# Keys, values and context of the first layer moved beside the edge checks, and the last layer's matrices loaded inside the edge loop of a graph transformer

## The chip, the cores and the metric

The kernel runs on one core of one Trainium2 chip. The metric is the device time of one execution in microseconds (us); lower is better. Engines are called by short names: PE is TensorE, DVE is VectorE, ACT is ScalarE, POOL is GpSimd and SP is SyncE, which here only issues transfers.

## The reference

Four layers work on 3125 nodes of 256 features with 103125 directed edges (`src`, `dst`, sorted by `dst`). Each layer adds a graph attention, a global mixing and an expert network:

```python
xn = layernorm(x)
x = x + gnn_i(xn, src, dst) + mix_i(xn)
x = x + ffn_i(layernorm(x))
```

The change touches the mixing and the edge attention of layer 0 and the expert network of layer 3:

```python
# layer 0, mixing: linear attention with a gate
q, k, v = split(x @ Wqkv)                      # 8 heads of 32
k = softmax(k, over the nodes)
context = einsum('nhd,nhv->hdv', k, v)
out = einsum('nhd,hdv->nhv', q, context)
gate = sigmoid(gelu((layernorm(x) * g + b) @ Wg1 + bg1) @ Wg2 + bg2)
mix = out * gate @ Wproj + bproj
# layer 0, edges: softmax over the edges of a target of leaky_relu(s_src[src] + s_trg[dst]),
# weighted sum of proj[src]
# layer 3, experts: one of 8 by the largest gate
H = gelu(x @ W1 + b1)                          # 1024 features
probs = softmax(H @ Wg + bg)
out[n] = probs[n, e] * (H[n] @ Wd[e] + bd[e])  # e = argmax(probs[n])
```

`Wd` is 8 matrices of 1024 x 256, 8.4 MB in f32.

## The kernel before

Nodes lie in 25 tiles of 125 (`NT`, `TP`), with 7 groups of three or four tiles (`GROUPS`). `x`, its layernorm `xn` and the transposed `xT` stay on chip through the whole kernel. All matrices are f32.

**Start.** `begin_layer` loads and normalises `x` group by group on DVE and ACT and turns it on PE. Then `prepare` checks whether the edges have the properties that the fast path needs (segments of the edge list per node block, sortedness, a bound on the attention exponents): five scans of 3224 numbers over `heads` on DVE (L1357), their addresses `at_i` (L1360), five indirect gathers on POOL, a DVE chain on the gathered segments, and matmuls `p_e` on every group of `xT` for the bounds of the attention scores. It ends in one number, `ok`, which every engine reads to choose a branch (`layers` or `general`). Only then does layer 0's real work start.

**Layer 0.** The attention of layers 0 to 2 is done densely, by a matrix of edge counts, `count_d`, in DRAM. `counts` makes it in 63 steps: per step DVE builds two one-hot tensors (`oh_lo` L1491, `oh_key` L1494), PE multiplies them into `p_cnt` and ACT copies the counts to a stage that SP stores. Between the steps it draws pieces of other work from a generator, so many that `PIECES0` pieces are spread over the steps:

```python
while done < (g0 // B + 1) * PIECES0 // steps:
    next(work, None)
    done += 1
```

What is left over follows after the last step. The pieces come from `mix0_pieces`, in this order: the loads of layer 0's weights and a POOL addition of `bproj` to all of `x`; 25 pieces of keys, values and context (per tile a product `p_a` with half of `Wqkv`, an exponential `ek` and a copy `v` on ACT, a column of ones on POOL, and two products into the running `p_ctx`); the folding of the context into the query matrix (`fold`); per group a normalised `xnn`, its turned `xnnT` with `ln_g` and `ln_b` (DVE, L1576), the gate (L1592) and the projection, added to `x` (L1599); then `node_pieces` for the edge attention's node terms: `hg` and its store `q_g`, `zs` and `es`, the exponentials `bar` and `es`, and last the scaling of `zs` by `es` on DVE. The dense attention (`pt` L1675, `acc`) then reads `count_d` and `q_g` back (`a`, `q_head`).

**Layer 3.** Its attention goes edge by edge in 101 steps (`edge_attention`): gathers of source rows on POOL, row and edge data on SP, one-hot products on PE. It too draws pieces: first the mixing `mix3`, then for each group the hidden layer `hidden3`, which writes each node's 1024 hidden features to `hid_d`. After the loop `routed3` loads `w_d`, one transfer an expert on SP, sorts the nodes by expert (`route`, whose result is `node_of`), gathers tiles of 128 nodes of one expert (`hid_tile` L2244), turns them (`p_t`) and multiplies by the expert's matrix (`p_q`).

The order of work on each engine is the order of the program, with the tiles' buffers as the only other limit.

Of the kernel before, what the change touches and what calls it, by code (L numbers as in the profile page):

```python
# [10 lines left out]
F32 = mybir.dt.float32  # L11
# [4 lines left out]
AF = mybir.ActivationFunctionType  # L16
OP = mybir.AluOpType
AX = mybir.AxisListType
PSUM = bass.MemoryType.PSUM
DRAM = bass.MemoryType.DRAM  # L20

P = 128
N = 3125
TP = 125
NT = N // TP
C = 256
KC = C // P
# [14 lines left out]
KEYS = HI * GN  # L42
PIECES0 = 107
SC = 8
# [5 lines left out]
GROUPS = [(0, 4), (4, 4), (8, 4), (12, 4), (16, 3), (19, 3), (22, 3)]  # L50
# [1276 lines left out]
class Dense(Net):  # L1327
# [8 lines left out]
    def prepare(self, pool, xT):  # L1336
# [6 lines left out]
        with ExitStack() as s:  # L1343
# [18 lines left out]
            for b in range(GN):  # L1362
                nc.gpsimd.indirect_dma_start(out=seg[:, b, :], out_offset=None, in_=ins["segments"],
                                             in_offset=bass.IndirectOffsetOnAxis(ap=at_i[:, b:b + 1], axis=0))
            lo = w.tile([TP, GN, SEG], F32, name="seg_lo")
            key = w.tile([TP, GN, SEG], F32, name="seg_key")
# [37 lines left out]
            nc.vector.tensor_reduce(found[:, 1:2], above, AX.X, OP.add)  # L1404
            p_f = ps.tile([1, 2], F32, name="p_f")
            nc.tensor.matmul(p_f, self.ones[:, 0:1], found, start=True, stop=True)


            gw = self.gnn_weight(w, ps, "g0", 8)
            ends = w.tile([16, 2, len(GROUPS)], F32, name="ends")  # L1410
# [30 lines left out]
            nc.vector.tensor_mul(self.ok, ok[:, 0:1], ok[:, 2:3])  # L1441
        return self.ok

# [4 lines left out]
    def counts(self, pieces):  # L1448
# [5 lines left out]
        with ExitStack() as s:  # L1454
# [5 lines left out]
            with tc.tile_pool(name="cnti", bufs=1) as wi, tc.tile_pool(name="cntt", bufs=2, space=PSUM) as ps:  # L1460
                for i, name in enumerate(("lo_t", "key_t")):
# [12 lines left out]
                    by_edge.append(t)  # L1474
            ps = s.enter_context(tc.tile_pool(name="cntp", bufs=3, space=PSUM))
            lo_t, key_t = by_edge
# [42 lines left out]
    def mix0_pieces(self, x, xn, xT, nodes, c, w):  # L1519
# [3 lines left out]
        with ExitStack() as s:  # L1523
            ps = s.enter_context(tc.tile_pool(name="m0p", bufs=3, space=PSUM))
            ps1 = s.enter_context(tc.tile_pool(name="m0p1", bufs=1, space=PSUM))
            wqkv = self.weight(c, "L0_mix_Wqkv")
            wproj = self.weight(c, "L0_mix_Wproj")
# [3 lines left out]
            bg1, bg2 = self.vec(c, "L0_mix_bg1", rows=64), self.vec(c, "L0_mix_bg2")  # L1531
            bproj = self.row(c, "L0_mix_bproj")
            nc.gpsimd.tensor_add(x, x, bproj[:, None, :].to_broadcast([TP, NT, C]))
            p_ctx = [ps1.tile([P, P + 1], F32, name=f"p_ctx{m}") for m in range(KC)]
            yield
            for t in range(NT):
                p = ps.tile([TP, 2 * C], F32, name="p_a")
                self.mm(p, [(xT[:, k, t * TP:(t + 1) * TP], wqkv[:, k, C:]) for k in range(KC)])
                ek = w.tile([TP, C], F32, name="ek", bufs=2)
                nc.scalar.activation(ek, p[:, :C], AF.Exp)  # L1540
                v = w.tile([TP, KC, P + 1], F32, name="v", bufs=2)
                nc.scalar.activation(v[:, :, :P], p[:, C:].rearrange("p (m f) -> p m f", m=KC), AF.Copy)
                nc.gpsimd.memset(v[:, :, P], 1.0)
                for m in range(KC):
                    nc.tensor.matmul(p_ctx[m], ek[:, m * P:(m + 1) * P], v[:, m, :], start=(t == 0), stop=(t == NT - 1))
                yield

            inv = w.tile([P, KC], F32, name="inv")
            ctxt = w.tile([P, KC, P], F32, name="ctxt")
            for m in range(KC):  # L1550
                nc.vector.reciprocal(inv[:, m:m + 1], p_ctx[m][:, P:])
                nc.vector.scalar_tensor_tensor(ctxt[:, m, :], p_ctx[m][:, :P], inv[:, m:m + 1], self.heads, op0=OP.mult, op1=OP.mult)
            fold = c.tile([P, KC, C], F32, name="fold")
            for k in range(KC):
                p = ps.tile([P, 512], F32, name="p_a")
                for m in range(KC):
                    nc.tensor.transpose(p[:, m * P:(m + 1) * P], wqkv[:, k, m * P:(m + 1) * P], self.ident)
                wt = w.tile([P, C], F32, name="wq_t")
                nc.vector.tensor_copy(wt, p[:, :C])
                p = ps.tile([P, 512], F32, name="p_a")  # L1560
                for m in range(KC):
                    nc.tensor.matmul(p[:, m * P:(m + 1) * P], wt[:, m * P:(m + 1) * P], ctxt[:, m, :], start=True, stop=True)
                nc.vector.tensor_copy(fold[:, k, :], p[:, :C])
            yield
            for t0, nt in GROUPS:
# [6 lines left out]
                for k in range(KC):  # L1572
                    p = ps.tile([P, 512], F32, name="p_a")
                    for t in range(nt):
                        nc.tensor.transpose(p[:, t * TP:(t + 1) * TP], xnn[:, t, k * P:(k + 1) * P], self.ident[:TP, :TP])
                    nc.vector.tensor_scalar(xnnT[:, k, :n], p[:, :n], g[:, k:k + 1], b[:, k:k + 1], op0=OP.mult, op1=OP.add)  # L1576
                yield
# [580 lines left out]

    def hidden3(self, w, ps, x, xn, xT, t0, nt, weights, ones, hid_d):

# [4 lines left out]
        n = nt * TP  # L2165
        cs = slice(t0 * TP, t0 * TP + n)
        mv = w.tile([TP, nt, 2], F32, name="mv")
# [7 lines left out]
        for t in range(nt):  # L2175
            nc.vector.tensor_scalar(xn[:, t0 + t, :], x[:, t0 + t, :], mv[:, t, 0:1], rstd[:, t:t + 1],
                                    op0=OP.subtract, op1=OP.mult)
        yield
        for k in range(KC):
            p = ps.tile([P, 512], F32, name="p_h")  # L2180
            for t in range(nt):
                nc.tensor.transpose(p[:, t * TP:(t + 1) * TP], xn[:, t0 + t, k * P:(k + 1) * P], self.ident[:TP, :TP])
            nc.scalar.activation(xT[:, k, cs], p[:, :n], AF.Copy)
            yield
        h = w.tile([P, F, 3 * TP], F32, name="h")
        for f in range(F):
            p = ps.tile([P, 512], F32, name="p_h")
            self.mm(p[:, :n], [(w1[:, k, f * P:(f + 1) * P], xT[:, k, cs]) for k in range(KC)])
            nc.scalar.activation(h[:, f, :n], p[:, :n], AF.Gelu, bias=b1[:, f:f + 1], scale=1.0)
            if f % 2:  # L2190
                yield
# [29 lines left out]

    def routed3(self, ones, hid_d, out):

# [6 lines left out]
        with ExitStack() as s:  # L2230
            c = s.enter_context(tc.tile_pool(name="r3", bufs=1))
            wd = c.tile([P, F, E, C], F32, name="w_d")
            for e in range(E):
                nc.sync.dma_start(wd[:, :, e, :], self.ins["L3_ffn_Wd"][e].rearrange("(k p) f -> p k f", p=P))
            bd = self.matrix_rows(c, "L3_ffn_bd")
            node, to, mats = self.route(c, ones, NJ)
            wd2 = wd.rearrange("p k e f -> p k (e f)")
            w = s.enter_context(tc.tile_pool(name="r3x", bufs=3))
# [17 lines left out]
            def products(j):  # L2256
                mat[j] = nc.values_load(mats[0:1, j:j + 1], engines=(mybir.EngineType.PE, mybir.EngineType.DVE), min_val=0, max_val=(E - 1) * C)
                q = ps.tile([P, C], F32, name="p_q")
                self.mm(q, [(hts[j][:, f, :], wd2[:, f, bass.ds(mat[j], C)]) for f in range(F)])
                y = w.tile([P, C], F32, name="y_tile")  # L2260
                nc.vector.tensor_add(y, q, bd[:, bass.ds(mat[j], C)])
                nc.vector.scalar_tensor_tensor(y, y, hrs[j][:, HID:HID + 1], hrs[j][:, HID + 1:], op0=OP.mult, op1=OP.add)
                self.scatter(y_d, to, j, y, "y3")
# [155 lines left out]
    def run(self, x_in, out):  # L2419
# [3 lines left out]
        x = pool.tile([TP, NT, C], F32, name="x")  # L2423
        xn = pool.tile([TP, NT, C], F32, name="xn")
        xT = pool.tile([P, KC, N], F32, name="xT")
# [3 lines left out]
        out_v = out.rearrange("(t p) c -> p t c", p=TP)  # L2429
        self.begin_layer(x, xn, xT)  # L2430
        ok = nc.values_load(self.prepare(pool, xT)[0:1, 0:1], min_val=0, max_val=1)
        with tc.If(ok > 0) as either:
# [4 lines left out]
    def layers(self, x, xn, xT, out):  # L2437
# [32 lines left out]
        with tc.tile_pool(name="layer3", bufs=1) as lp:  # L2470
            ones = lp.tile([TP, NT, 8], BF16, name="one_e")
            hid_d = self.dram.tile([N, HID + 1 + C], F32, name="hid_d")
            with tc.tile_pool(name="edges", bufs=1) as ep:
                with tc.tile_pool(name="ffn2", bufs=1) as wp:
# [6 lines left out]
                self.edge_attention(  # L2481
                    x, xT, edge, lambda w, ps: self.mix3(w, ps, x, xn, xT, mix),
                    lambda w, ps, t0, nt: self.hidden3(w, ps, x, xn, xT, t0, nt, hid, ones, hid_d))
            self.routed3(ones, hid_d, out)

# [127 lines left out]
```

## Time and profile before

| | us |
|---|---|
| median of 3 runs | 5581.91 (5577.47 to 5591.57) |
| the profiled execution | 5581.36, its span 5579.3 |
| PE busy | 4887.1 (88%) |
| DVE busy | 3778.7 (68%) |
| ACT busy, POOL busy | 1037.5 and 1038.3 (19% each) |
| start to the branch on `ok` | 93.9 |
| first and last step of the counting | 131.3 to 385.4 |
| first `pt` of the dense attention | 406.33 |
| edge loop of layer 3 | 4299 to 5361 |
| first `p_q` of layer 3's experts | 5418.31 |

The granted clock of PE was 0.935 on average. Busy times are sums over the whole span; a share of 88% is an average over stages that have different limits, so the rows below it, the places where one stage ends and the next starts, are what a change to one stage is read against. A row of the timeline gives start, length, engine, line, operation and tiles, and in brackets how long the engine was idle before it and what released it.

### The profile page before, as it was taken

What the parts mean: (1) busy time and instruction counts of PE and PEld (TensorE: products, weight loads), DVE (VectorE), ACT (ScalarE), POOL (GpSimd) and SP (SyncE); (2) the same over time, 40 slices, a digit from 0 to 9 for tenths busy, and PEclk for the clock granted to TensorE, in tenths of its full rate; (3) what the DMA queues carried; (4) which work ended last, traced back from release to release, by engine and by line L of the source; (5) the groups of instructions that cost most, each with busy time, mean ns of one, the idle gap of its engine ahead of it and who ended that gap; (6) DMA issues with size and microseconds to landing.
All of it is one profiled execution on the core that took longest, in us unless ns stands there. A gap on an engine that the chain in (4) does not pass through costs nothing. (4 is left out here: it accounts for less than half of the span.)

```text
span 5579.3 us, 66975 instructions
## 1 busy us (share of the span) xinstructions
PE 4887.1 (88%) x24880; PEld 2854.4 (51%) x24880; DVE 3778.7 (68%) x6022; ACT 1037.5 (19%) x1991; POOL 1038.3 (19%) x1184
## 2 busy tenths in 40 slices
PE   3978888879698899999999899979998888988868
PEld 2652234448555433378544433345565556655557
DVE  7789999975555699745443899932223888777743
ACT  2540010011143100100123000023233112332221
POOL 1000000004200000000001100000001777767733
PEclk7989999979899999999889999979999889999989
DMA  3462222232300011111000011120002556666655
GB/s 87 35 69 66 77 63 66 67 114 65 111 1 1 29 34 41 30 41 36 19 1 4 28 33 34 33 63 0 1 0 65 158 156 179 180 167 169 179 168 170
DMA packets 294389, 395.84 MB, mean 71 GB/s; under 512 B 124223, under 2 KB 228048, under 8 KB 293483
## 3 DMA queue, kind: packets, MB, share of 16 engines
q1 hardware_dynamic: 205646, 163.34, 12.5%
q0 software_dynamic: 52528, 167.17, 10.6%
q10 hardware_dynamic: 35882, 60.93, 3.4%
q8 instruction: 203, 3.33, 0.3%
q14 instruction: 130, 1.06, 0.1%
HBM read 345.14 MB, written 49.35 MB: 71 GB/s over the span
## 5 line engine op out<-in xcount | busy, mean ns | idle before, releaser
L1675 DVE SCALAR_TENSOR_TENSOR pt<-q_head,bar,a 128x750 f32<-128x750 f32 (+5 forms) x1200 | 1483.5, 1299 | 80.3 <-PE acc L1780 57.3
L1930 POOL DMA_INDIRECT z_edge<-tab,src_i x806 | 775.0, 962 | 274.5 <-issue 207.9
L1724 PE MATMUL acc<-pt,zs 128*64 128x500 f32 (+2 forms) x2800 | 592.1, 549 | 150.7 <-DVE pt L1675 126.7
L1775 PE MATMUL acc<-pt,zs 128*64 128x375 f32 (+2 forms) x3200 | 605.9, 502 | 25.2 <-DVE pt L1675 24.9
L1998 PE MATMUL p_acc<-z_edge,oh 128*125 128x264 f32 x2044 | 542.4, 427 | 94.9 <-DVE z_edge L1989 94.8
L1998 PEld LDWEIGHTS p_acc<-z_edge,oh 128*125 128x125 f32 x2044 | 421.1, 210 | 195.3 <-DVE z_edge L1989 105.1
L1724 PEld LDWEIGHTS acc<-pt,zs 128*64 128x64 f32 (+1 forms) x2800 | 244.8, 137 | 482.7 <-DVE pt L1675 327.0
L1775 PEld LDWEIGHTS acc<-pt,zs 128*64 128x64 f32 (+1 forms) x3200 | 245.1, 136 | 362.7 <-issue 224.5
L1191 DVE SCALAR_TENSOR_TENSOR x<-p_y,sm,x 125x256 f32<-125x256 f32 x200 | 93.9, 484 | 428.2 <-PE p_y L716 428.2
L1780 PE MATMUL acc<-pt,zs 128*32 128x375 f32 (+2 forms) x3200 | 313.4, 497 | 0.0
L1826 PE MATMUL acc<-zs,pt 128*125 128x257 f32 x1250 | 275.7, 383 | 11.6 <-issue 11.6
L1826 PEld LDWEIGHTS acc<-zs,pt 128*125 128x125 f32 x1250 | 234.8, 189 | 52.5 <-issue 14.4
L1989 DVE TENSOR_TENSOR z_edge<-z_edge,near_e 128x2112 f32<-128x2112 f32 (+1 forms) x101 | 236.6, 2342 | 16.7 <-ACT near_e L1981 16.7
L1186 ACT ACTIVATE h<-p_tr,bn 128x500 f32<-128x500 f32 (+1 forms) x224 | 161.5, 722 | 361.1 <-PE p_tr L716 361.1
L716 PE MATMUL p_y<-w_L_ffn_Wo,h 128*125 128x256 f32 x800 | 203.7, 387 | 0.0
L1675 DVE SCALAR_TENSOR_TENSOR pt<-q_all,bar,a 128x500 f32<-128x500 f32 (+3 forms) x175 | 119.1, 682 | 122.6 <-PE acc L1826 120.3
L1622 POOL MEMSET es<- 128x4 f32 (+2 forms) x4 | 1.6, 400 | 1052.1 <-PE acc L1780 723.3
L716 PE MATMUL p_tr<-h,w_L_ffn_W 128*128 128x500 f32 (+1 forms) x448 | 191.7, 551 | 6.3 <-ACT h L1186 3.2
L716 PE MATMUL p_tr<-xT,w_L_ffn_W 128*128 128x500 f32 (+1 forms) x448 | 193.0, 554 | 0.0
L2315 POOL CAST one_e<-one 125x96 bf16<-125x96 f32 (+1 forms) x2 | 2.1, 1047 | 1014.0 <-DVE one L653 1014.0
L1780 PEld LDWEIGHTS acc<-pt,zs 128*32 128x32 f32 (+1 forms) x3200 | 85.0, 109 | 203.1 <-issue 201.8
L716 PEld LDWEIGHTS p_y<-w_L_ffn_Wo,h 128*125 128x125 f32 x800 | 144.9, 187 | 73.5 <-ACT h L1186 27.1
(505 smaller groups left out, 6998.5 us busy)
## 6 DMA issues: line engine op xcount, KB each, us to landing
row<-dst_row SPq DMA_DIRECT2D x101, 224.0 KB
a<-count_d SPq DMA_DIRECT2D x96, 203.1 KB
a<-count_d SPq DMA_DIRECT2D x96, 187.5 KB
a<-count_d SPq DMA_DIRECT2D x144, 93.8 KB
ef<-in_edge_s SPq DMA_DIRECT2D x101, 128.0 KB
z_edge<-tab,src_i POOLq DMA_INDIRECT x806
count_d<-stage SPq DMA_DIRECT2D x12, 781.2 KB
q_head<-q_g ACTq DMA_DIRECT2D x24, 375.0 KB
```

Source lines behind the costliest of these rows:

```text
L716: self.nc.tensor.matmul(p, a, b, start=(i == 0), stop=(i == len(pairs) - 1))
L1186: nc.scalar.activation(o[:, m, :n], p[:, :n], AF.Relu, bias=b[:, e, m:m + 1], scale=g[:, e, m:m + 1])
L1191: nc.vector.scalar_tensor_tensor(x[:, t0 + t, :], q, wf[:, t, e:e + 1], x[:, t0 + t, :], op0=OP.mult, op1=OP.add)
L1675: self.nc.vector.scalar_tensor_tensor(pt[:K, :n], q, bar, a[:K, :n], op0=OP.max, op1=OP.mult)
L1724: nc.tensor.matmul(acc[64 * i:64 * i + 64, :b1 - b0], zs[:K, t, z:z + 64], pts[i][:K, b0:b1], start=(t == 0), stop=(t == NS - 1))
L1775: nc.tensor.matmul(acc[i // 2][64 * (i % 2):64 * (i % 2) + 64, b, :b1 - b0], zs[:K, t, i * W:i * W + 64], pts[i][:K, b0:b1], **st)
L1780: nc.tensor.matmul(acc[2][32 * i:32 * i + 32, b, :b1 - b0], zs[:K, t, z:z + 32], pts[i][:K, b0:b1], **st)
L1826: nc.tensor.matmul(acc[i], pt[:K, i * TP:(i + 1) * TP], zs[:K, t, :C + 1], start=(t == 0), stop=(t == NS - 1))
L1930: nc.gpsimd.indirect_dma_start(out=zs[i][:, j, :], out_offset=None, in_=table, in_offset=bass.IndirectOffsetOnAxis(ap=src[:, c0 + j:c0 + j ...
L1989: nc.vector.tensor_mul(zh, zh, weight[:, :, :, None].to_broadcast([P, n, H, D + 1]))
L1998: nc.tensor.matmul(acc[t], ohs[i, t][:, k - a, :], zs[i][:, k - c0, :HW], start=(k == cols[t][0]), stop=(k == cols[t][1] - 1))
L2315: nc.gpsimd.tensor_copy(ones[:, 0, ts, :], one1)
```

## The change

There are two independent parts.

1. Layer 0's keys, values, context and fold move into a new function, `begin`, ahead of the branch: `begin_layer` is gone from the start, and each group's layernorm, turning and key/value products follow each other, while `prepare` becomes a generator that stops twice, once behind the segment gathers and once ahead of its last matmuls. The fold goes through DRAM (`fold_d`) to the pieces. `PIECES0` falls from 107 to 69, while the pieces fall from 107 to 81, so that the last twelve (the end of `node_pieces`) follow the counting. `xnnT` is written by ACT instead of DVE, and two PSUM pools get four buffers instead of three.
2. `Wd` is loaded in eight parts by rows of 128 hidden features (1 MB each) instead of by expert. Five of them go on SP inside the edge loop, as ten more pieces behind `mix3`, into the space of `xT` and `xn`; `hidden3` uses a small remainder of `xn` for its own normalised and turned tiles. The other three follow in `routed3`, two on ACT's queue and one on SP's, and the bias `bd` behind them.

```diff
-PIECES0 = 107
+PIECES0 = 69
...
                 nc.gpsimd.indirect_dma_start(out=seg[:, b, :], out_offset=None, in_=ins["segments"],
                                              in_offset=bass.IndirectOffsetOnAxis(ap=at_i[:, b:b + 1], axis=0))
+            yield
...
             nc.vector.tensor_reduce(found[:, 1:2], above, AX.X, OP.add)
+            yield
-            p_f = ps.tile([1, 2], F32, name="p_f")
+            p_f = ps.tile([1, 2], F32, name="p_e")
...
+    def begin(self, pool, x, xn, xT):
...
+            checks = self.prepare(pool, xT)
+            next(checks)
+            wqkv = self.weight(c, "L0_mix_Wqkv")
+            p_ctx = [ps1.tile([P, P + 1], F32, name=f"p_ctx{m}") for m in range(KC)]
+            self.layernorm(xn, x, GROUPS[0])
+            for i, (t0, nt) in enumerate(GROUPS):
+                self.transposed(pst, xT, xn, groups=[GROUPS[i]])
+                if i + 1 < len(GROUPS):
+                    self.layernorm(xn, x, GROUPS[i + 1])
+                if i == 2:
+                    next(checks)
+                for t in range(t0, t0 + nt):
+                    p = ps.tile([TP, 2 * C], F32, name="p_a")
+                    self.mm(p, [(xT[:, k, t * TP:(t + 1) * TP], wqkv[:, k, C:]) for k in range(KC)])
+                    ek = w.tile([TP, C], F32, name="ek")
+                    nc.scalar.activation(ek, p[:, :C], AF.Exp)
+                    v = w.tile([TP, KC, P + 1], F32, name="v")
+                    nc.scalar.activation(v[:, :, :P], p[:, C:].rearrange("p (m f) -> p m f", m=KC), AF.Copy)
+                    nc.gpsimd.memset(v[:, :, P], 1.0)
+                    for m in range(KC):
+                        nc.tensor.matmul(p_ctx[m], ek[:, m * P:(m + 1) * P], v[:, m, :], start=(t == 0), stop=(t == NT - 1))
...
+            nc.sync.dma_start(self.fold_d, fold.rearrange("p k f -> p (k f)"))
+            for _ in checks:
+                pass
...
-            ps = s.enter_context(tc.tile_pool(name="cntp", bufs=3, space=PSUM))
+            ps = s.enter_context(tc.tile_pool(name="cntp", bufs=4, space=PSUM))
...
-            ps = s.enter_context(tc.tile_pool(name="m0p", bufs=3, space=PSUM))
-            ps1 = s.enter_context(tc.tile_pool(name="m0p1", bufs=1, space=PSUM))
-            wqkv = self.weight(c, "L0_mix_Wqkv")
+            ps = s.enter_context(tc.tile_pool(name="m0p", bufs=4, space=PSUM))
...
+            fold = c.tile([P, KC, C], F32, name="fold")
+            nc.sync.dma_start(fold.rearrange("p k f -> p (k f)"), self.fold_d)
...
-                    nc.vector.tensor_scalar(xnnT[:, k, :n], p[:, :n], g[:, k:k + 1], b[:, k:k + 1], op0=OP.mult, op1=OP.add)
+                    nc.scalar.activation(xnnT[:, k, :n], p[:, :n], AF.Identity, bias=b[:, k:k + 1], scale=g[:, k:k + 1])
...
+    def part3(self, queue, out, f):
+        queue.dma_start(out.rearrange("p (e c) -> p e c", c=C), self.ins["L3_ffn_Wd"][:, f * P:(f + 1) * P, :].rearrange("e p c -> p e c"))
...
+    def pieces3(self, w, ps, x, xn, xT, mix, parts):
+        yield from self.mix3(w, ps, x, xn, xT, mix)
+        for f, o in enumerate(parts):
+            self.part3(self.nc.sync, o, f)
+            yield
+            yield
...
-            wd = c.tile([P, F, E, C], F32, name="w_d")
-            for e in range(E):
-                nc.sync.dma_start(wd[:, :, e, :], self.ins["L3_ffn_Wd"][e].rearrange("(k p) f -> p k f", p=P))
+            more = c.tile([P, F - len(parts), E * C], F32, name="w_d")
+            wd = list(parts)
+            for f in range(len(parts), F):
+                wd.append(more[:, f - len(parts), :])
+                self.part3(nc.scalar if f % 2 else nc.sync, wd[f], f)
```

## The prediction

> **What bounds the kernel now.** I read the windows over the start of the program first, because two thirds of the diff lies there. The columns after the length are busy us (and rows) of PE, PEld, DVE, ACT, POOL, then the granted clock, the DMA share and GB/s.
>
> ```profile
> core 0: us, PE busy (x) PEld busy (x) DVE busy (x) ACT busy (x) POOL busy (x), PEclk, DMA share, GB/s
> 14.00:55.00 41.00, 12.20 (x59) 9.67 (x60) 40.92 (x82) 4.88 (x11) 0.29 (x1) 0.62 0.30 70
> 55.00:67.00 12.00, 6.60 (x12) 1.18 (x10) 1.77 (x4) 0.00 (x0) 6.24 (x5) 0.78 0.38 107
> 67.00:93.00 26.00, 9.15 (x24) 2.13 (x24) 22.18 (x43) 0.00 (x0) 0.00 (x0) 0.63 0.15 49
> ...
> 131.20:197.00 65.80, 64.19 (x474) 43.47 (x473) 43.89 (x34) 39.33 (x95) 1.92 (x19) 1.00 0.44 35
> ...
> 205.00:320.00 115.00, 108.03 (x729) 74.58 (x727) 98.84 (x112) 61.55 (x105) 0.00 (x0) 0.97 0.46 36
> 320.00:385.50 65.50, 62.94 (x548) 47.51 (x546) 58.76 (x70) 42.32 (x99) 0.00 (x0) 1.00 0.61 49
> ```
>
> Until the branch at 93.9 us VectorE is the bound (40.92 of 41 us), then the segment gathers (POOL 6.24 of 12), then VectorE; TensorE works 28 of 93 us. In the counting from 131.2 on, TensorE is full while keys and values are interleaved (64.19 of 65.8); afterwards TensorE and VectorE are both near full (98.84 of 115 on VectorE). So TensorE work can move from a full stage to an empty one, if the empty one's order lets it.
>
> The timeline of single engines shows that order and the two ends that the diff touches.
>
> ```profile
> 53.30 0.99 DVE L1404 TENSOR_REDUCE found<-col_lo 128x1 f32<-128x806 f32 x1
> 54.21 0.17 DVE L1360 TENSOR_SCALAR at_i<-at 125x5 int32<-125x5 f32 x1
> ...
> 66.61 1.49 DVE L1368 CAST rel<-seg 125x1280 f32<-125x1280 int32 x1 [7.30 <-DMA seg<-in_segments,at_i]
> ```
>
> ```profile
> 109.36 13.68 POOL L1533 TENSOR_TENSOR x<-x,r_L_mix_bproj 125x6400 f32<-125x6400 f32 x1 [12.81 <-DMA r_L_mix_bproj<-in_L_mix_bproj]
> 122.98 0.14 POOL L1543 MEMSET v<- 125x2 f32 x2
> ```
>
> ```profile
> 392.92 0.17 DVE L644 TENSOR_SCALAR back<-iota 125x8 f32<-125x8 f32 x1
> 406.33 1.78 DVE L1675 SCALAR_TENSOR_TENSOR pt<-q_head,bar,a 128x1500 f32<-128x1500 f32 x1 [13.24 <-DMA a<-count_d]
> ```
>
> ```profile
> 5379.54 23.34 SPq L2234 DMA_DIRECT2D w_d<-in_L_ffn_Wd  x8
> ...
> 5395.72 0.18 DVE L2148 CAST node_of<-at_n 128x32 int32<-128x32 f32 x1
> ...
> 5401.95 1.03 POOL L2244 DMA_INDIRECT hid_tile<-hid_d,node_of  x1 [36.19 <-DMA w_d<-in_L_ffn_Wd]
> ```
>
> ```profile
> 5409.86 3.89 PE L2250 MATMUL p_t<-ident,hid_tile 128*128 128x128 f32 x16 [14.85 <-DMA hid_tile<-hid_d,node_of]
> 5418.31 6.55 PE L716 MATMUL p_q<-w_d,hid_t 128*128 x16 [4.56 <-DMA w_d<-in_L_ffn_Wd]
> ```
>
> To be seen: the gathers' addresses are ready at 54.21 and their data at 66.61; a POOL addition holds POOL until 122.98; dense attention starts at 406.33 on a transfer, with VectorE idle for 13.24 us; in layer 3 the last stage starts behind 8.4 MB of matrices.
>
> **The change, part by part.** The sum is made against the profiled run, 5581.36 us (span 5579.3 and 2.1 around it), 0.55 below the median 5581.91. Its steps are those of begin, counting, handover and last stage.
>
> *Begin stage, +34 (bounds +20 and +47).* Keys, values and context of 25 tiles move ahead of the branch. A tile's four p_a rows (0.48 apart) and four p_ctx rows (0.52 together) occupy TensorE for 2.4 us, as in the interleaved stage. In the new order POOL sets v's ones column for three tiles, then issues the five gathers, then sets 21 more. The gathers wait for at_i, so p_ctx of the fourth tile waits for them, and with two buffers for ek, v and p_a everything behind it. VectorE gets its five scans (3.57 each) earlier, since the later groups' layernorm stands behind them: I put at_i at 47.5 instead of 54.2, and the last gather's issue 7.9 later, as now, at 55.4. Two p_a tiles are ahead by then. Left on TensorE: 22 p_ctx x 0.52 = 11.4, 41 halves of p_a x 0.93 = 38.1, 18 transposes x 0.155 = 2.8, and 2.5 for a slow clock at the start, with waits 57: end at 112. Then fold (two reciprocals and scalings, 4 transposes, 8 products, four copies: some 4 us by their rows around 200), and, since the order puts all 14 remaining checks' matmuls behind the last tile, the p_e chain, which in this trace runs from 81.57 to ok at 92.66, 11.1. Branch 1.2 later: 128 instead of 93.9. VectorE's segment chain (66.6 to 80.8) is covered by that. Lower end: the p_ctx wait costs TensorE nothing that it would not have idled (the kv work starts near 30): 114. Upper: the p_e chain is serial at the slow clock and each group loses 2 us: 141.
>
> Weighed here: the new order alternates square root and exponential four times. The trace has that table load at 1283 ns (eight before 150 us), and at 125.69 the next exponential starts 1.29 after the load's start. The Trainium skill, "ScalarE: Activation LUTs", section "What ACT_TABLE_LOAD costs", counts the drain too, about 2.66 us a switch. Three of the four pairs fall before 55, in the wait for the gathers. The fourth stands ahead of two tiles' ek: by the row 2.6 us, by the rule 5.3, against 4.8 us of p_a ahead on TensorE. By the row it costs nothing, by the rule half a microsecond; I take the row.
>
> *Counting, -44 (bounds -36 and -52).* From the branch to the first p_cnt the work is the same: seg_in, its turns, and the POOL addition, which still stands before the second one-hot: 37.4 before, 37.5 taken. The fold's reload (0.26 MB on SP) replaces the load of wqkv there. Now 63 steps remain with 69 slots for 81 pieces; without kv TensorE has about 176 us of work, VectorE more. VectorE: 61 steps x 2.79 (oh_lo to oh_lo, 363.30 and 366.23, less the es between them) = 170; 14 additions to x, 8.8; 14 gate products, 7.3; the normalisations behind the first count 5.7; rest 3.5: 195. xnnT, 14 rows of 0.79 or 0.66, goes from VectorE to ACT, which has room (61.55 of 115). VectorE idles 16 of 115 and 7 of 65.5 us there now, waiting for p_a mostly; a fourth PSUM buffer for each pool shortens some, and I keep 14. Last count 37.5 + 195 + 14 + 2 = 248 behind the branch, against 291.5 now. Lower gain: all waits stay in proportion (22): -36. Higher: the buffers take most away: -52.
>
> *Handover, +5 (0 to +7).* Twelve pieces are left behind the counting: six or seven node tiles, the last q_g store, bar, es, and four scalings. In ACT's order the DMA issue of q_head, which waits for q_g's store, stands ahead of the exponentials of bar and es; and zs's scaling on VectorE (24 rows, 384.8 to 392.8, 8.2 us), now hidden in the wait of 13.24 for the counts, comes behind es. From last store to first pt is 20.9 us now (385.4 to 406.33); the transfers take 15.5 to the issue of a. Then es 0.5, scaling 8.2 and sync 1: about 26. If ACT doesn't wait for q_g, the scaling is done first: 0.
>
> *Last stage, -13 (-17 to -6).* Five of eight parts of Wd (1 MB each) go on SP in the edge loop into space that the turned x and normalised x leave. There the DMA share is 0.68, 188 GB/s (window 4800 to 4900), for some 1060 us; 5.2 MB more is 5 GB/s. The row loads queued behind them on SP are fetched two steps (21 us) ahead, and each part waits for the last mixing read of its space, which by the trace's rows of the mixing falls within some 7 us of SP's place: no cost that the chain sees; bounds -3 and +6, as a late row load would stop the loop for a part of a step. At the end 3.1 MB are left instead of 8.4: at the 341 GB/s seen there 9 us, so by 5390. hid_row, which waited 8.89 for space on ACT, is free sooner, node_of at 5395.72 becomes the last wait of the first gather, 5396 instead of 5401.95. Its landing and turning took 7.9 and 4 us with the queue full; the p_q stall of 4.56 goes: first p_q at 5405 instead of 5418.31. The bias, 1 MB now last in ACT's queue, is first needed behind p_q. If the gather is as slow, 5408; if the bias is late, 5412.
>
> Sum: +34 - 44 + 5 - 13 = -18: 5563.
>
> **The rivals.** *A, kv is nearly free beside the checks.* For it: 65 idle TensorE microseconds before 93.9. Against it: the POOL order above and the checks' products placed last. If POOL's issue doesn't hold p_ctx, kv runs from about 32 and the branch falls at 114: +20 - 44 + 3 - 13 = -34: 5547.
>
> *B, slower: the begin stage outgrows what the counting gives back.* One mechanism: TensorE's stop-and-go. Every tile waits for ek and v through two buffers, the clock stays where it is in this stage (0.62), and p_a rows cost 0.83 to 1.19, as p_e's and p_a's do there, instead of 0.59. 22 tiles x 2.4 x 0.6 = +32 on top of the forecast: 5595. It decides from +18 upward for no gain, +35 for slower by more than 0.3%; so it needs nearly the whole stage slow. Against it: the p_e rows of this trace speed up from 54.5 on within 5 us of dense work, and the interleaved kv has clock 1.00. The Trainium skill, "TensorE: Matmul & The Clock Gate", section "What's actually happening", gives the reason: half speed until about 3.4 us of sustained work; by it a stall must recur, which one tile's 0.8 us of ek and v cannot make with two tiles of p_a ahead. By the row (0.62) the stage would be +32, by the rule +2; I take the rule's side because the kv work is dense.
>
> *C, the matrices gain nothing.* The last stage then starts on hid_d and bias, or a part on SP blocks row loads: 0 for -13: 5576, and up to 5582 with a late row.
>
> **How the numbers follow.** Forecast 0.55 (own range 5551 to 5577), A 0.20, B 0.12, C 0.13. The median of this kernel moves by some 0.25% between runs, so 0.3%, 17 us, is what a measurement can tell; the line is at 5565. Faster: 0.64 of the forecast and all of A, 0.55. Slower: three quarters of B, 0.09. Same: 0.36. Range for 8 in 10: most of A down to 5541, up to 5586, leaving out most of B.
>
> **What would show it.** Right: ok's read near 127; a POOL idle of over 10 us before the first gather and PE waiting on v or ek until 55; first p_cnt near 166, last count store near 376; first pt near 402, its idle naming ACT or VectorE's own scaling instead of the transfer; xnnT as ACT rows; the first gather released by node_of and p_q at once behind hid_t. Wrong: the branch before 115 (A) or after 146 with clock under 0.7 (B); VectorE waits on p_a above 22 us in the counting; edge-loop steps above 10.5 us; p_q still waiting on a transfer (C).

## The result, and the profile after

The changed kernel takes 5551.19 us (median of five runs, 5548.36 to 5563.13) against 5585.53 for the kernel before (five runs, 5577.47 to 5592.18): ratio 0.9944, 95% interval 0.9927 to 0.9961. Measured again (the run `e11_after_again` below) it takes 5540.22 against 5575.25, ratio 0.9936 (0.9922 to 0.9950). That is 34 and 35 us, faster by 0.6%; 18 had been forecast, and 5563 lay 12 us above the measured median.

The profiled execution of the changed kernel was the slowest of its five runs, 5563.13 with a span of 5561.3, so the two traces differ by 18 us only. Read by stages they show where the rest is.

| us | before | after | difference | forecast |
|---|---|---|---|---|
| start to the last step of `ok` | 92.66 | 123.98 | +31 | +34 |
| `ok` to the first p_cnt | 38.6 | 41.7 | +3 | 0 |
| first p_cnt to the issue of the last count store | 254.1 | 199.3 | -55 | -44 |
| last count store to the first pt | 20.9 | 27.1 | +6 | +5 |
| first pt to the start of the edge loop's last p_acc | 4954.8 | 4967.9 | +13 | 0 |
| from there to the first p_q | 57.2 | 46.6 | -11 | -13 |
| first p_q to the end of the span | 161.0 | 154.7 | -6 | 0 |

The five rows that the forecast named give -25 in this pair of traces; with the marks of `e11_after_again` in place of the first trace's they give -33. The row of +13 is no cost of the change. It lies in layers 0 to 2, whose code is unchanged: from the first pt to the first p_acc this trace takes 3932 us, the kernel before 3914 and the repeated run 3913, while the edge loop, with the five loads in it, is 5 us shorter than before. From the first pt to the last p_acc it is 4946.2 in the repeated run, and 4944 to 4955 in seven edited ones (the other four ran on a chip where the edge loop is longer). So it is the drift of one execution (mean granted clock 0.935 in that run, 0.937 to 0.940 in the other four). The -6 of the last row is no gain of the change either: `e1_layer0_only`, whose layer 3 is as before, takes 156.4 there.

The windows of the changed kernel (busy us and rows of PE, PEld, DVE, ACT, POOL; granted clock; DMA share; GB/s):

```profile
core 0: us, PE busy (x) PEld busy (x) DVE busy (x) ACT busy (x) POOL busy (x), PEclk, DMA share, GB/s
14.00:55.00 41.00, 24.54 (x78) 13.95 (x78) 38.00 (x70) 15.36 (x27) 5.94 (x7) 0.82 0.40 102
55.00:67.00 12.00, 11.12 (x34) 6.29 (x34) 7.12 (x7) 3.40 (x8) 1.72 (x7) 0.75 0.28 85
67.00:93.00 26.00, 25.57 (x89) 12.23 (x89) 8.28 (x15) 6.74 (x21) 1.11 (x11) 1.00 0.11 35
93.00:125.30 32.30, 28.49 (x107) 11.88 (x105) 13.56 (x41) 4.33 (x13) 0.40 (x4) 1.00 0.02 9
125.30:166.00 40.70, 17.57 (x57) 8.71 (x58) 35.61 (x74) 14.81 (x31) 16.23 (x4) 0.62 0.29 72
166.00:280.00 114.00, 106.85 (x901) 78.32 (x899) 110.34 (x106) 75.28 (x140) 0.00 (x0) 0.97 0.59 43
```

TensorE, which worked 9.15 of 26 us between 67 and 93, now works 25.57, at the full granted clock. In the counting VectorE is busy 110.34 of 114 us: it was held by TensorE before and is the bound now. The waits say the same; first the counting before (131.3 to 385.4), then the changed kernel (166 to 372):

```profile
DVE oh_lo L1491 <- PE p_cnt L1506: 31.1, 19, 5.5
DVE x L1599 <- PE p_a L716: 6.7, 6, 1.7
DVE gate L1592 <- PE p_a L716: 6.0, 7, 2.2
```

```profile
DVE es L1667 <- ACT zs L1666: 6.4, 5, 3.5
DVE oh_lo L1546 <- PE p_cnt L1561: 4.6, 2, 2.5
DVE x L1624 <- PE p_a L716: 1.1, 1, 1.1
```

The columns behind the colon are us in all, times and the longest. Of 31.1 us in which the one-hots waited for TensorE, 4.6 are left, and of the 6.4 behind `zs` 5.9 lie after the last count.

The places that the forecast named, in the timelines of the changed kernel, the start first:

```profile
47.55 0.17 DVE L1360 TENSOR_SCALAR at_i<-at 125x5 int32<-125x5 f32 x1
...
59.88 1.49 DVE L1369 CAST rel<-seg 125x1280 f32<-125x1280 int32 x1 [7.32 <-DMA seg<-in_segments,at_i]
```

```profile
54.46 1.21 POOL L1363 DMA_INDIRECT seg<-in_segments,at_i  x1 [0.30 <-issue]
55.67 0.16 POOL L1475 MEMSET v<- 125x2 f32 x2
...
137.88 13.80 POOL L1588 TENSOR_TENSOR x<-x,r_L_mix_bproj 125x6400 f32<-125x6400 f32 x1 [9.94 <-DMA r_L_mix_bproj<-in_L_mix_bproj]
```

```profile
138.08 14.39 DVE L619 TENSOR_SCALAR xnn<-xn,mv,rstd 125x256 f32<-125x256 f32 x3
```

```profile
39.93 0.30 ACT L616 ACTIVATE rstd<-mv,eps 125x3 f32<-125x3 f32 x1 [5.59 <-DVE mv L614]
40.24 1.28 ACT L1472 ACT_TABLE_LOAD   x1
41.54 0.38 ACT L1472 ACTIVATE ek<-p_a 125x256 f32<-125x256 f32 x1
```

```profile
42.34 1.20 PE L1477 MATMUL p_ctx<-v,ek 125*128 125x129 f32 x4 [5.66 <-ACT v L1474]
...
55.84 1.23 PE L1477 MATMUL p_ctx<-v,ek 125*128 125x129 f32 x4 [5.84 <-POOL v L1475]
...
107.30 0.68 PE L1477 MATMUL p_ctx<-v,ek 125*128 125x129 f32 x4
...
121.69 0.29 PE L1424 MATMUL p_e<-ident,both_ends 16*1 16x16 f32 x2 [1.15 <-DVE both_ends L1419]
```

The addresses are ready at 47.55, POOL issues the last gather at 54.46, the memset behind it at 55.67 releases p_ctx at 55.84. From there TensorE is dense to 107.98, and the checks' products follow. It had waited before: at 42.34 for ACT, whose exponential `ek` (41.54) stood behind a square root `rstd` (39.93) that waited for VectorE. Behind the branch the POOL addition (137.88) holds VectorE's normalisation (138.08). In the kernel before, the same addition (109.36) held the second one-hot on VectorE, two rows that take 2.83 us without it:

```profile
113.88 11.87 DVE L1494 TENSOR_TENSOR oh_key<-key_t,is_key 128x2520 bf16<-128x2520 bf16 x2 [3.48 <-ACT key_t L1473]
```

At the other ends:

```profile
383.73 0.27 DVE L1671 TENSOR_SCALAR es<-es 128x200 f32<-128x200 f32 x1 [14.15 <-ACT es L1670]
...
392.10 20.39 DVE L1700 SCALAR_TENSOR_TENSOR pt<-q_head,bar,a 128x1500 f32<-128x1500 f32 x12
```

```profile
5394.94 0.18 DVE L2173 CAST node_of<-at_n 128x32 int32<-128x32 f32 x1
```

```profile
5396.95 1.03 POOL L2292 DMA_INDIRECT hid_tile<-hid_d,node_of  x1 [32.28 <-DMA m_L_ffn_bd<-in_L_ffn_bd]
```

```profile
5402.13 1.94 PE L2298 MATMUL p_t<-ident,hid_tile 128*128 128x128 f32 x8 [7.89 <-DMA hid_tile<-hid_d,node_of]
...
5406.63 1.56 PE L716 MATMUL p_q<-xT,hid_t 128*128 x6 [0.20 <-issue]
```

Before the attention, VectorE's idle time now names ACT's `es`, and the scaling of `zs` stands between it and the first pt. In layer 3 the first gather follows `node_of` by 2 us and p_q no longer waits for a matrix. The gather's row, though, names the transfer of the bias and not `node_of`, as it does in all twelve runs with this part. Whether it waited for the bias, or for the stores of `hid_d` that stand ahead of it on ACT's queue, no run separates.

### The profile page after: what moved, and what is told of

Read it like the earlier page. It is cut to its first block, busy times and chain, and to the rows that moved or that the text cites. A ratio compares the mean times of both kernels' runs of the same rounds, so it can differ in the third digit from the quotient of the medians.

```text
span 5561.3 us, 66940 instructions
## 1 busy us (share of the span) xinstructions
PE 4908.2 (88%) x24880; PEld 2861.3 (51%) x24880; DVE 3770.7 (68%) x6008; ACT 1050.8 (19%) x2007; POOL 1038.7 (19%) x1184
## 3 DMA queue, kind: packets, MB, share of 16 engines
q0 software_dynamic: 52528, 167.17, 10.6%
## 4 chain that ended last, share of the span: by engine, by line
PE 58%; DVE 20%; issue 10%; POOL 5%; DMA 4%; ACT 2%; ACTq 0%; DVEq 0%; SPq 0%; POOLq 0%
PE acc L1800 10%; DVE pt L1700 9%; PE p_tr L716 8%; PE p_acc L2023 6%; PE acc L1805 5%; PE acc L1851 5%; PE p_y L716 5%; PE p_a L716 3%; POOL z_edge L1955 3%; PE p_h L716 2%; PE p_q L716 2%; PE p_kvt L716 2%; PE acc L1749 1%; PE p_t L716 1%; DVE z_edge L2014 1%
## 5 line engine op out<-in xcount | busy, mean ns | idle before, releaser
L716 PEld LDWEIGHTS p_y<-w_L_ffn_Wo,h 128*125 128x125 f32 x800 | 144.9, 187 | 73.4 <-ACT h L1186 27.1
```

The source lines that it names most:

```text
L716: self.nc.tensor.matmul(p, a, b, start=(i == 0), stop=(i == len(pairs) - 1))
```

## The experiments

They ran on three chips. Times are compared on one chip, with the kernel before; the changed kernel itself ran beside e9, e10 and e12 only, so e1 to e8 are compared with it by stages. The ratios are taken over all runs and need not equal the quotient of the medians.

**The two parts alone.** `e1_layer0_only` has layer 0's part with layer 3 of before, `e2_matrices_only` the reverse:

```diff
...
-    x, xT, edge, lambda w, ps: self.pieces3(w, ps, x, xn, xT, mix, room[0]),
-    lambda w, ps, t0, nt: self.hidden3(w, ps, x, room, t0, nt, hid, ones, hid_d))
-self.routed3(ones, hid_d, room[0], out)
+    x, xT, edge, lambda w, ps: self.mix3(w, ps, x, xn, xT, mix),
+    lambda w, ps, t0, nt: self.hidden3(w, ps, x, xn, xT, t0, nt, hid, ones, hid_d))
+self.routed3(ones, hid_d, out)
```

> Layer 0's part of the change alone; layer 3 as before. Theory (the two parts add, and nothing between them reacts): branch near 125, first p_cnt near 166, last count store near 365 and first pt near 392, as in the changed kernel, 14 us before the old 406; from the end of the edge loop to the first p_q 57 us as before; time 14 us under before. Rival (the loads of the matrices in the edge loop cost time there that only the end gives back): the edge loop is some 5 us shorter than in the changed kernel, time 20 us under before.

> Layer 3's part alone; layer 0 as before. Theory: the start is as before (first pt 406), from the end of the edge loop to the first p_q some 46.5 us instead of 57, no start of the products at a slow clock (3 us), a shorter end (3 us): 14 to 17 us under before. Rival (the edge loop pays for the loads): the loop from first gather to last p_acc takes over 1066 us against 1061, and the time is less than 10 us under before.

On this chip the kernel before takes 5871.86 us. e1: 5855.63, ratio 0.9960 (0.9944 to 0.9977), 16 us less. e2: 5851.38, ratio 0.9960 (0.9934 to 0.9986), 20 us less. The sum of both, 36, is near what the whole change gives elsewhere (34 and 35). The intervals, 13 to 33 us and 8 to 39 us, are too wide to show more than that each part gains by itself.

By stages, e1 has its last count store at 365.3 and its first pt at 387.8, and 57.6 us from the last p_acc to the first p_q; e2 has 46.9 there, and starts the counting at 130.2 as the kernel before does. But e2's first pt is at 398.1, 8 us earlier than in the trace of the kernel before, with the same code of layer 0; 5 of the 8 lie in the counting (249.0 us for 254.1). So a mark of one trace carries an error of some us: from e2 to e1 the first pt comes 10 us earlier, from the kernel before to the changed one 14, to e11 21.

The edge loop (first to last p_acc) took 1337.5 in e1, without the loads, and 1320.6, 1329.7 and 1342.8 in e2, e3 and e4, with them; on the other chips 1041.0 in the kernel before and 1033 to 1042 with the loads. The rival asked for 5 us more with the loads, and nothing of that kind stands out of this spread. The 3 us each of a slow start and a longer end, expected of e2, did not show: from the first p_q to the end it took 158.2, e1 156.4.

**Pieces behind the counting, and xnnT.**

```diff
-PIECES0 = 69
+PIECES0 = 81
```

> The changed kernel with PIECES0 = 81, so that no piece is left behind the counting. Theory (the counting is bound by VectorE, and the twelve pieces bring it only es copies of 0.16): last count store later by 1 to 4 us (366 to 369), es and zs scaled within the wait for the counts, first pt 21 us behind the store, so at 387 to 390 against 392.1: 2 to 5 us faster than the changed kernel. Rival (TensorE's 0.9 us a piece and ACT's copies push the steps over VectorE's pace): last store 8 us later or more, first pt at 394 or later, no gain.

```diff
-nc.scalar.activation(xnnT[:, k, :n], p[:, :n], AF.Identity, bias=b[:, k:k + 1], scale=g[:, k:k + 1])
+nc.vector.tensor_scalar(xnnT[:, k, :n], p[:, :n], g[:, k:k + 1], b[:, k:k + 1], op0=OP.mult, op1=OP.add)
```

> The changed kernel with xnnT written by VectorE again (14 rows of 0.66 to 0.79). Theory (VectorE bounds the counting): last count store 8 to 10 us later, at 373 to 375, time 8 to 10 us above the changed kernel. Rival (TensorE bounds it; PE waited 4.1 us for ACT's xnnT): the last store moves by less than 3 us either way.

Both ran on the same chip as e1 and e2. e3: 5823.04, ratio 0.9899 (0.9877 to 0.9922), last count store at 366.5, first pt at 382.0, 15.5 behind it; the changed kernel's pt is at 392.1 in its first trace and at 385.0 in the second. So leaving the twelve pieces behind the counting saves 1 to 4 us there and costs 7 to 12 at the handover, 3 to 10 in all. In part this is the stores: with no q_g store behind the last count store, SP issues the first `a` 10.2 us behind it, against 12.5 to 17.5 with the twelve pieces left. The whole time of e3 was lower than that step explains: its edge loop happened to be shorter than e4's (1329.7 and 1342.8). e4: 5856.5, ratio 0.9951 (0.9924 to 0.9979); its last count store is at 374.2, 9 us later than e1's with xnnT on ACT, and 8 of the 9 lie behind the first p_cnt. Its time fits as well (e1 lacks the 11 us of layer 3, e4 the 9 us of xnnT, and the medians are equal within 1 us), but the runs of each spread over 30 us or more, so the stage mark is the evidence. VectorE bounds the counting.

**The begin stage.** First the column of ones, then the checks, then the addition of `bproj`:

```diff
+vs = [c.tile([TP, KC, P + 1], F32, name=f"v{i}") for i in range(2)]
+for v in vs:
+    nc.gpsimd.memset(v[:, :, P], 1.0)
 checks = self.prepare(pool, xT)
...
-v = w.tile([TP, KC, P + 1], F32, name="v")
+v = vs[t % 2]
...
-nc.gpsimd.memset(v[:, :, P], 1.0)
```

> The changed kernel with the column of ones of v set once, in two fixed buffers, ahead of the gathers, so that no memset of POOL stands behind them. Theory (POOL's order holds p_ctx of the fourth tile until the gathers are issued): the wait of 5.84 us at 55.8 goes, the last p_ctx and the branch come 5 to 7 us earlier (102 and 119), and so does the first pt. Rival (ACT's order, in which ek of the next tiles stands behind the rstd of later groups and so behind VectorE's scans, holds the tiles as well): the stall stays under another name and the branch moves by 0 to 2 us.

e5: 5534.69 against 5589.53, ratio 0.9914 (0.9893 to 0.9935). `ok` at 116.4 (7.6 us earlier), first p_cnt at 158.7, last store at 356.6, first pt at 378.7. The wait for POOL was real. What is left is the rival's, and the changed kernel has it too, at 42.34: in e5 TensorE waits 6.7 us for ACT's `v`, since ek of later tiles stands behind the square roots of later groups, which wait for VectorE's scans.

```profile
PE p_ctx L1479 <- ACT v L1477: 6.7, 3, 3.8
```

```diff
 if i == 2:
     next(checks)
+if i == len(GROUPS) - 1:
+    for _ in checks:
+        pass
```

> The changed kernel with the rest of the checks (p_e and what follows) ahead of the last group's three tiles instead of behind the fold. Theory (the tail behind the last tile, 107.98 to 123.98, is a chain of TensorE and VectorE steps, of which TensorE's own share is about 12): its end chain and the fold's waits overlap with the tiles' work, branch 3 to 5 us earlier. Rival (the chain's length is TensorE's work alone, or the reads of the branch wait for the fold): no change within 1 us.

e6: 5541.92, ratio 0.9929 (0.9906 to 0.9951). `ok` came 6.6 us earlier, at 117.4, but the first p_cnt at 166.7, 1 us later. TensorE takes the branch in its own order: the last tiles and the fold now stand ahead of it, to 122.9. An early `ok` is worth nothing here, since the work around it is TensorE's in any case. The first row behind the branch:

```profile
130.82 1.27 PE L1529 MATMUL p_t<-ident,seg_in 125*128 125x125 f32 x4 [7.94 <-DMA seg_in<-seg_d]
```

For the third, the branch of general inputs adds no `bproj` of its own any more:

```diff
...
+    if t > 4:
+        for u in range(NT * (t - 5) // 20, NT * (t - 4) // 20):
+            nc.gpsimd.tensor_add(x[:, u, :], x[:, u, :], bproj)
...
-nc.gpsimd.tensor_add(x, x, bproj[:, None, :].to_broadcast([TP, NT, C]))
```

> The changed kernel with the addition of bproj to x made on POOL in 25 pieces beside the later keys and values, instead of in one of 13.8 us between the branch and the first p_cnt. Theory (that addition holds VectorE's normalisation, 14.39 instead of some 1.2 us, and with it the whole start of the counting): from the branch to the first p_cnt 28 to 30 us instead of 40, last count store and first pt 10 to 12 us earlier; the begin stage is not longer by more than 2. Rival (the loads and turns of the segments hold the start as well): 4 us or less.

e7: 5533.52, ratio 0.9909 (0.9888 to 0.9931). From `ok` to the first p_cnt it is 29.4 us, as the theory has it, against 41.7. But `ok` itself is at 133.0, 9 us late: sixteen of the 25 additions were placed at the very start, beside VectorE's busiest stretch, and at_i moved from 47.5 to 53.7. Left over: first p_cnt at 162.5.

```profile
17.59 9.39 POOL L1480 TENSOR_TENSOR x<-x,r_L_mix_bproj 125x256 f32<-125x256 f32 x12 [13.10 <-DMA r_L_mix_bproj<-in_L_mix_bproj]
27.38 3.73 POOL L1480 TENSOR_TENSOR x<-x,r_L_mix_bproj 125x256 f32<-125x256 f32 x4 [0.40 <-DVE xn L619]
```

**The handover.**

```diff
-nc.scalar.dma_start(qs[i][:, :n], dview(q_d, (h0 + i) * N + d0, [[0, P], [1, n]]))
+nc.sync.dma_start(qs[i][:, :n], dview(q_d, (h0 + i) * N + d0, [[0, P], [1, n]]))
```

> The changed kernel with the q_head loads of layer 0 on SP's queue instead of ACT's, so that ACT's exponentials of bar and es do not stand behind an issue that waits for the q_g stores. Theory: the exponentials run at 370 right behind the last node tile, es and zs are scaled by 379 within the wait for the counts, and the first pt follows the landing of a: 16 to 20 us behind the last count store instead of 27 (22.5 in other runs of the same code). Rival (the landing of the counts sets it anyway): 22 us or more.

e8: 5537.98, ratio 0.9916 (0.9895 to 0.9937). `es` is scaled at 366.89 and `zs` done at 375.2, and the first pt, 20.0 behind the last count store, names the transfer again:

```profile
375.04 0.18 DVE L1676 COPY zs<-es 128x25 f32<-128x25 f32 x1
381.51 13.62 DVE L1700 SCALAR_TENSOR_TENSOR pt<-q_head,bar,a 128x1500 f32<-128x1500 f32 x8 [6.28 <-DMA a<-count_d]
```

So the issue of q_head on ACT's queue did hold the exponentials. It cost 2 to 3 us: with that order unchanged the step took 22.1 to 23.1 in seven traces, and without it 20.0 here and 20.4 in e10. The 27.1 of the first trace is longer for another reason. Its q_head, which waits for the stores, was issued 17.4 us behind the last count store; in the seven it was 12.4 to 13.4. Why the stores landed later there stays open.

**All together, the change again, and its buffers.** e9 joins the early ones, 81 slots and a `bproj` addition that waits for a value of the segment chain (about 76 us); e10 has 69 slots and q_head on SP instead.

```diff
+self.zero = pool.tile([TP, 1], F32, name="zero_seg")
+nc.vector.tensor_scalar(self.zero, found[:TP, 0:1], 0.0, None, op0=OP.mult)
...
+nc.vector.tensor_scalar(late, bproj, self.zero[:, 0:1], None, op0=OP.add)
...
+            nc.gpsimd.tensor_add(x[:, u, :], x[:, u, :], late)
```

> The changed kernel with three of the earlier edits together: ones set once, PIECES0 = 81, and the addition of bproj on POOL in 25 pieces that wait for the end of the segment chain (about 74), when VectorE is idle. Theory (the three stalls lie one behind the other, so their gains add): branch near 117 as in the run with the early ones, 30 us from ok to the first p_cnt, so first p_cnt near 146, last count store near 343, first pt 16 to 21 behind it, near 361: about 30 us faster than the changed kernel. Rival (they share a wait, such as the segments' loads or TensorE's own work): 15 us or less.

> As the run before, but with PIECES0 = 69 and the q_head loads on SP instead. Theory: the same start, last count store near 342, first pt 20 behind it, near 362: 28 to 30 us faster than the changed kernel. Rival: 13 us or less.

> The changed kernel itself, to be compared on one chip with the others. Theory: 25 to 35 us under before; branch 124, first p_cnt 166, last count store 365, first pt 388 to 392. Rival (the first measurement's 34 us was part chance): 15 to 20.

On this chip the kernel before takes 5575.25. e11, the changed kernel: 5540.22, ratio 0.9936 (0.9922 to 0.9950). e9: 5521.53, ratio 0.9900 (0.9884 to 0.9915). e10: 5520.89, ratio 0.9901 (0.9885 to 0.9916). Both are 19 us faster than the changed kernel, the best versions here, and their first pt stands at 365.6, 19.4 us ahead of e11's 385.0. The gains add, though not to 30. From e11 to e9, `ok` comes 3.2 us earlier (119.9), and not 7 as in e5, since at_i came 2.2 later. From `ok` to the first p_cnt 13.0 are saved (41.8 to 28.8); the counting is 3.5 longer (198.1 to 201.6); the handover is 6.7 shorter (22.1 to 15.4). And the expectation counted from a first pt of 392, which was the long handover of one trace. The additions, off VectorE's way, now end long before the branch:

```profile
76.42 17.23 POOL L1486 TENSOR_TENSOR x<-x,late_bias 125x256 f32<-125x256 f32 x25 [18.87 <-DVE late_bias L1474]
```

```diff
-ps = s.enter_context(tc.tile_pool(name="cntp", bufs=4, space=PSUM))
+ps = s.enter_context(tc.tile_pool(name="cntp", bufs=3, space=PSUM))
-ps = s.enter_context(tc.tile_pool(name="m0p", bufs=4, space=PSUM))
+ps = s.enter_context(tc.tile_pool(name="m0p", bufs=3, space=PSUM))
```

> The changed kernel with three buffers in the two PSUM pools of the counting, as before. Theory (the fourth buffer took away what VectorE still waited for TensorE in the counting, which the prediction put at 14 us): VectorE's idle time in the counting rises from 13 to 20 us or more and the last count store comes 5 to 8 us later, 370 to 373. Rival (without the keys and values TensorE is ahead anyway): within 2 us of 365.

e12: 5539.25, ratio 0.9926 (0.9913 to 0.9940), last count store at 361.7 against e11's 362.9, and VectorE idle in the counting for 6.9 us against 7.6. The rival is right: the fourth buffers are worth nothing.

## Why the prediction was right, and where its sizes were off

- *Begin stage, +34.* Measured +31.3. at_i at 47.55 was foreseen at 47.5, the end of the gathers at 55.67 for 55.4, and the mechanism, POOL's order, was shown by e5. The last p_ctx ended at 107.98 for 112, mostly because the working had one tile too few ahead of the gathers. It let POOL set three columns of ones before them and 21 behind, which makes 24 of 25 tiles. In the trace four stand before them, the last at 34.25; so it is the fifth tile that waited, and by then six tiles had their p_a, not four and a half. At the working's own rates this is 3.3 us less to do. (`begin` writes the gathers ahead of all tiles, so the order on an engine is not simply that of the program's text; it has to be read from a trace.) Rival A, a branch at 114, needed POOL out of the way; e5 did that and reached 116.4.
- *Table loads.* Rows of 1.28 us again (at 40.24, and the exponential at 41.54, 1.30 later), not the 2.66 of the Trainium skill's "ScalarE: Activation LUTs", section "What ACT_TABLE_LOAD costs"; and from the end of the wait for POOL to 121 TensorE waits for nothing. What the pairs did cost is another thing, which the working did not have: the square roots wait for VectorE's scans, and ek behind them. In the changed kernel they came ahead of the wait for POOL, which hid what they cost until e5.
- *Clock.* Rival B's slow clock did not come: 1.00 from 67 on. Behind the wait, p_ctx rows of four took 1.23 at 55.84 and 0.68 from 67; the p_a rows came to full pace within some 5 us, by an estimate from two that took 1.91 at 56.86 and six that took 3.53 at 59.43 and 2.74 at 64.50. This is the side that the prediction took.
- *Counting, -44.* This is the mis-sized term: from `ok` to the last store it measured 241.0 for 292.8 before, -51.7 in all, made of +3.1 ahead of the first p_cnt and -54.8 behind it. From the first p_cnt on the working has 195 us of VectorE's work, 14 of waits and 2 at the end, 211 in all. Measured are 190.3, 7.5 and 1.5, together 199.3. So the waits were put at nearly twice their size, and the work some 5 us too high. (VectorE's waits to 372 are 13.4, near the 14, but 5.9 of them lie behind the last count.) The reason given for shorter waits, a fourth buffer, is wrong (e12): without the keys and values VectorE seldom waits for TensorE with three buffers either. That VectorE is the bound is shown by e4. The 241.0 is firm (241.0 again in e1, 239.8 in e11); the 292.8 less so (287.9 in e2, with the same code), so the gain is 47 to 52.
- *From the branch to the first p_cnt, 0.* Measured +3. The working took the work there as unchanged, and it is not. The POOL addition starts 13.9 us behind `ok` instead of 16.7 and lasts as long. Before, it held the second one-hot on VectorE, and the first p_cnt followed 8.2 us behind its end. Now it holds three normalisation rows for 14.39 us, and the first group's turning, gate and projection stand between them and the first p_cnt: 14.0 us. The prediction left the addition in place; e7 and e9 show that it was worth 12 to 13 us.
- *Handover, +5.* Measured +6 in the first trace and +1 to +2 in seven others. The mechanism, ACT's order, is shown by e8; the size hangs on the stores. The working took 15.5 us to the issue of `a`; it was 17.5 in the first trace and 12.5 to 13.5 in the others.
- *Last stage, -13.* Measured -10.6 to the first p_q, by the way that was named: p_q 11.7 us earlier, without its stall. One sign is half missed: the first gather stood at 2 us behind node_of, but its row names the bias. Rival C falls with e2: 46.9 us instead of 57.6.
- *The sum.* -18 was forecast, and -18 is what the two profiled executions show, but by chance: there a drift of +13 in unchanged work hides what the touched stages gave. The medians, -34 and -35, are the measure. They stand near rival A's 5547 and at the lower edge of the forecast's own range (5551), and yet not by A's way, since the branch came at 125 and not at 114. With the marks of e11 the stages give -33, and of the 15 us beyond the forecast 12 lie in the counting and 4 each in the begin stage and the handover, less 3 and 2 in the other two.

## What to carry to other kernels

Work moved from a stage that its engine bounds into one where that engine idles is paid at the price of the new stage's order, not at zero: here 31 us of 55 came back as a longer start, some 7 of them because one tiny memset stood behind five gathers in a queue. Ask of each moved instruction what stands ahead of it on its own engine, on all engines that feed it. And take the gain of a stage from stage marks in several traces: the same code differed by 8 us at the first pt and by 13 us between first pt and last p_acc.

## What the runs showed that was not expected

A POOL addition of 125 x 6400 (13.80 us) holds three VectorE normalisation rows for 14.39 us; three rows of the same form at 51.03 took 1.07. In pieces at the start (13.1 us of POOL work in 16 pieces by 31) it put at_i 6 us behind: there sixteen normalisation rows took 9.8 us that take 5.5 in the changed kernel. In 25 pieces from 76 to 94, where VectorE mostly idles, it cost nothing that shows: the one copy of xT inside took 0.55, as without it. The Trainium skill, "SBUF — State Buffer", section "Who interferes with whom", says that VectorE and GpSimd share a pair of ports and that, where a VectorE instruction needs it too, whoever issues first has the pair for the whole instruction and the other is blocked. The single long addition agrees with it: it began at 137.88, 0.2 us ahead of the three rows, and they ended 0.8 us behind it.

The chips differ in one stage: the edge loop took 1033 to 1042 us on two of them and 1321 to 1343 on the third, with the same code. Between 4700 and 4900 us POOL's gathers lasted as long each there (954 ns for 951), but there were 123 of them against 156. The cause stays open.
